# Two Mamba2-like mixers on one core: C·B by blocks, block totals by a product with ones, running sums of two chunks side by side

## The chip, the cores and the metric

The kernel runs on one core of a Trainium2 chip. The metric is the device time of one execution in microseconds (us), lower is better. The engines of the core work side by side, each through its own instructions in order: PE (TensorE, matrix products and transposes), DVE (VectorE), ACT (ScalarE), POOL (GpSimd) and SP (SyncE, which here only issues DMAs). All data are float32; a float32 product shows as two weight loads and two passes in the trace, a transpose as one of each.

## The reference

The input x is (4, 1024, 512): four sequences of 1024 rows. Four layers follow one another, each with a layer norm ahead of it and a residual around it: mixer a, a gated feed-forward layer (ffn), mixer b, the same ffn again.

```python
x = x + mixer_a(layernorm(x))
x = x + ffn(layernorm(x))
x = x + mixer_b(layernorm(x))
x = x + ffn(layernorm(x))
```

Both mixers project x to a gate z (1024 wide), to h (1024), B and C (N each) and to dt (one per head), convolve h, B and C over four rows, apply silu, and run a linear recurrence over the rows. Mixer a has 16 heads of 64 with a state of N = 64; mixer b has 64 heads of 16 with N = 128. The recurrence as mixer b has it:

```python
dt = softplus(dt + dt_bias)
a = -exp(A_log) * dt                 # per row and head; decay exp(a)
state = state * exp(a) + outer(dt * h, B)
y = state @ C + D * h
...
mixer_a: out = norm_w * rms_norm(y * silu(z)) @ out_proj
mixer_b: out = norm_w * rms_norm(y) * silu(z) @ out_proj
```

Mixer a's reference is already written in blocks of 64 rows: within a block y = ((C·Bᵀ) * L) @ (dt h), with L the exponentials of differences of the running sums of a; from block to block a state is carried, which decays by the exponential of the block's total of a.

## The kernel before

**Tiles.** The 4096 rows are 32 chunks of 128 (P), 8 (NCH) to a sequence. Two chunks (GC = 2) make a group, so each mixer has 16 groups. A chunk has two blocks (NQ = 2) of 64 rows (BL). Constants that differ: mixer a has NH = 16, N = 64, SH = P // N = 2, HP = 32, NE = 2·NH + NQ·NH/SH = 48; mixer b has NH = 64, N = 128, SH = 1, HP = 64, NE = 256.

**Order.** `mixer()` emits its work under a manual schedule: PE, DVE, ACT and POOL run exactly in the order in which the Python code emits, only SP's queue is arranged by a scheduler. The loop over groups steps through two generators: `chunk(f, c, following)` for the two chunks of the present group, and `front(ahead, behind)`, which projects the next group. A planner adds up the microseconds that `chunk` yields and emits pieces of `front` until they are paid.

**The pieces of front.** `gate(n)`, n = 0 to 7, projects z in halves of a PSUM bank; after each second one ACT takes a tanh (`tz`, L585), and DVE makes `z` (L590) when the list `later_on` is run, after the next piece. `convolve(j)` projects one tile of h, B or C for both chunks (259 columns, L389), ACT makes the first tap into `u` (L519), DVE adds three (L523); `silu` follows one piece later (tanh L530; L533 writes B as `Bc`, L537 C as `Cc`, L543 h). The first convolution pieces are those of B and C. From the seventh piece on each piece also takes one step of `softplus` (L593 to L651): the steps make dt, then `a` (L619, L620), then a split of `a` in a coarse and a fine part (`parts`, L627, L628), and two steps on the running sums `pcs` of both chunks (L633), their negative as float32 `ncs` and as float16 `two` (ACT, L644, L645), the rest of the float16 pair (DVE, L646), and four DMAs on SP's queue (L650).

**Small steps.** A list `small` holds small PE steps; `large` (L388) pops one behind each large projection product. `prologue(f, c)` puts 13 steps there for a chunk: `sums_of(0)` C·B into a PSUM tile `misc` (L796), `sums_of(1)` and `(2)` running sums of `a` within the block (products with the masks `le_b` and `gt_b`, L798), `sums_of(3)` the blocks' totals of `a` (products with the mask `block`, L805), `sums_of(4)` the transpose of B (L814), with ACT's `ea` = exp of all sums (L816) and the copy `Bt` (L818) and DVE's `Gm`, C·B under the causal mask (L822); then 8 transposes of h (L771), with DVE's dt·h (`hdt`, L775) and ACT's skip D·h (L789). The steps of a group's chunk 0 are deferred at `gate(7)` of the front before it, those of chunk 1 at the start of chunk 0.

**A chunk.** `chunk` makes on POOL the decayed copies of the state (L1005 with its kin), in `decays` the exponents of L by PE (`seg`, L862, L874) and their exponential by ACT (L886, tile `L_b` in mixer b); `weigh` multiplies by Gm on DVE (L893); `to_state` is PE's `pst` (L991) with DVE's additions to the carried states (`Sq` L1000 and L1002, `S` L1025) and POOL's decay between (L1010); `from_state` is PE's `po` (L930) and DVE's `yo` (L941); `open_y` turns yo back (L953), `inner` adds the inside of the blocks (L908), and `close_y` adds D·h (L971), gates on POOL (L977) and takes squares on ACT (L976, L980). `tail` is the output projection `pout` (L722), the sum of squares `ssq` (L731), a copy on ACT (L741) and the residual (L748).

PSUM in a mixer is one pool `mm` of eight banks, taken in rotation. In mixer b the last six groups also carry the end of the first ffn for their rows (`last_steps`). The weights' scaling `weigh_rows` runs on ACT behind the first front.

## Time and profile before

| | us |
|---|---|
| runs of the kernel before | 2763.74, 2763.35, 2756.45 (median 2763.35) |
| the profiled execution | 2760.33, its span 2758.5 |
| mixer a's middle, 60 to 1080 of the span (1020 us) | PE busy 985.5, DVE 747.0, ACT 388.5, POOL 284.7 |
| mixer b's middle, 1330 to 2520 (1190 us) | PE 1144.5, DVE 940.0, ACT 490.1, POOL 365.8 |
| one group of mixer a, 358.5 to 424.4 (65.9 us) | PE 64.0, DVE 48.7, ACT 25.4 |
| an early group of mixer b, 1658.4 to 1734.4 (76.0 us) | PE 75.1, DVE 59.5, ACT 32.0 |
| a late group of mixer b, 2132.3 to 2215.5 (83.2 us) | PE 76.1, DVE 67.1, ACT 33.3 |

The granted TensorE clock is 0.97 to 0.99 of full in the three long stretches. How to read the profile: a line of a timeline has the start in us from the start of the span, the time over which the instructions listed (xN) stretch, the engine, the line of the kernel, the operation, `output<-inputs` with their shapes, and in square brackets how long the engine had been idle just before and whose end released it. For PE the shape ahead of the sizes (`64*128`) is the tile of the array that is used, rows by columns. Pass ends on PE are modelled, so the intervals from start to start are the firmer number. A line of the waits names the waiting instruction, the releaser, the total of the idle time, the number of waits and the longest, in us. Names ending in `_a` and `_b` belong to the mixers, `_f` to the ffn.

### The profile page before, as it was taken

The page shows a single profiled execution, that of the slowest core. Times are in us where ns is not written, and L with a number is a line of the kernel's source. Part 1 is how long each engine was busy: PE and PEld are TensorE (multiplying, and loading weights), DVE is VectorE, ACT ScalarE, POOL GpSimd, SP SyncE. Part 2 cuts the span into 40 slices and gives each one's busy share as a digit, 9 for nine tenths or more (in the row PEclk, how much of TensorE's full clock was granted, in tenths as well). Part 3 has the DMA queues.
Part 4 walks back from the last instruction along what each step waited for, and adds up shares of the span by engine and source line. Part 5 has one row for each costly group of instructions (what it writes and reads, how often), then busy time and mean ns, then how long its engine had stood idle before and what let it go on. Part 6 is the DMA issues. An engine that isn't in the chain of part 4 may idle for free.

```text
span 2758.5 us, 59105 instructions
## 1 busy us (share of the span) xinstructions
PE 2613.9 (95%) x23636; PEld 1682.3 (61%) x23642; DVE 2006.6 (73%) x4493; ACT 1109.5 (40%) x2618; POOL 856.0 (31%) x955
## 2 busy tenths in 40 slices
PE   7999999999999998998999999999999998998897
PEld 6666666666666664345766666666666656665243
DVE  6677777777777775267877777778877778876359
ACT  3333333343433333355434434444434434333246
POOL 1222222222222223053232312322333323324049
PEclk9999999999999999999999999999999999999899
DMA  3000000000000004452000000000000000002424
GB/s 133 11 18 18 18 19 18 22 22 18 18 18 18 15 11 144 175 191 77 12 20 21 23 23 15 23 23 23 24 24 28 19 26 30 11 13 97 175 74 145
DMA packets 93009, 125.09 MB, mean 45 GB/s; under 512 B 38728, under 2 KB 42328, under 8 KB 92736
## 3 DMA queue, kind: packets, MB, share of 16 engines
q1 hardware_dynamic: 80960, 98.23, 11.0%
q10 hardware_dynamic: 9792, 16.82, 1.7%
q0 software_dynamic: 1984, 6.26, 0.7%
q8 instruction: 188, 3.08, 0.5%
q14 instruction: 85, 0.70, 0.1%
HBM read 84.54 MB, written 36.72 MB: 44 GB/s over the span
## 4 chain that ended last, share of the span: by engine, by line
PE 38%; DVE 17%; issue 2%; ACT 2%; POOL 1%; DMA 1%; SPq 0%; DVEq 0%; POOLq 0%; ACTq 0%
PE pc_b L389 7%; PE pz_b L389 7%; PE pout_b L722 6%; PE g_ps L1307 5%; DVE u_b L523 3%; PE py_b L908 2%; DVE L_b L893 2%; PE po_b L930 2%; PE pst_b L991 1%; PE d_ps L1262 1%; DVE no L1443 1%; PE seg_b L862 1%; PE d_ps L1229 1%; PE pd_b L552 1%; PE tph_b L771 1%
## 5 line engine op out<-in xcount | busy, mean ns | idle before, releaser
L389 PE MATMUL pc_b<-xnT_b,w_in_b 128*128 128x259 f32 x1280 | 349.2, 398 | 11.6 <-DVE h_b L971 9.0
L523 DVE SCALAR_TENSOR_TENSOR u_b<-pc_b,cw_b,u_b 128x256 f32<-128x256 f32 x480 | 231.7, 483 | 130.2 <-ACT u_b L519 118.3
L523 DVE SCALAR_TENSOR_TENSOR u_a<-pc_a,cw_a,u_a 128x256 f32<-128x256 f32 x432 | 208.6, 483 | 153.9 <-ACT u_a L519 142.5
L389 PE MATMUL pc_a<-xnT_a,w_in_a 128*128 128x259 f32 x1152 | 319.2, 400 | 0.0
L389 PE MATMUL pz_a<-xnT_a,w_in_a 128*128 128x256 f32 x1024 | 296.7, 406 | 13.3 <-DVE z_a L590 12.6
L389 PE MATMUL pz_b<-xnT_b,w_in_b 128*128 128x256 f32 x1024 | 292.6, 399 | 4.0 <-ACT xnT_b L485 4.0
L389 PEld LDWEIGHTS pc_b<-xnT_b,w_in_b 128*128 128x128 f32 x1280 | 220.9, 192 | 94.6 <-issue 36.5
L1307 PE MATMUL g_ps<-gw,xnT_f 128*128 128x512 f32 x512 | 246.9, 616 | 9.7 <-ACT xnT_f L1300 4.8
L389 PEld LDWEIGHTS pc_a<-xnT_a,w_in_a 128*128 128x128 f32 x1152 | 195.1, 190 | 73.7 <-ACT th_a L530 12.2
L722 PE MATMUL pout_b<-w_out_b,h_b 128*128 128x512 f32 x512 | 231.9, 607 | 0.4 <-POOL h_b L977 0.4
L722 PE MATMUL pout_a<-w_out_a,h_a 128*128 128x512 f32 x512 | 227.5, 597 | 1.0 <-POOL h_a L977 1.0
L389 PEld LDWEIGHTS pz_a<-xnT_a,w_in_a 128*128 128x128 f32 x1024 | 171.1, 193 | 60.2 <-issue 21.8
L389 PEld LDWEIGHTS pz_b<-xnT_b,w_in_b 128*128 128x128 f32 x1024 | 170.4, 192 | 43.8 <-issue 9.5
L977 POOL TENSOR_TENSOR h_b<-h_b,z_b 128x256 f32<-128x256 f32 x128 | 103.2, 827 | 289.1 <-ACT sq_b L976 289.1
L722 PEld LDWEIGHTS pout_b<-w_out_b,h_b 128*128 128x128 f32 x512 | 98.9, 196 | 112.9 <-issue 110.3
L1307 PEld LDWEIGHTS g_ps<-gw,xnT_f 128*128 128x128 f32 x512 | 92.2, 193 | 121.0 <-issue 107.9
L893 DVE TENSOR_TENSOR L_b<-L_b,Gm_b 128x1024 f32<-128x1024 f32 x128 | 163.9, 1322 | 1.0 <-ACT L_b L886 1.0
L519 ACT ACTIVATE u_a<-pc_a,cb_a,cw_a 128x256 f32<-128x256 f32 x144 | 80.7, 560 | 206.8 <-PE pc_a L389 206.8
L519 ACT ACTIVATE u_b<-pc_b,cb_b,cw_b 128x256 f32<-128x256 f32 x160 | 90.1, 563 | 183.1 <-PE pc_b L389 183.0
L722 PEld LDWEIGHTS pout_a<-w_out_a,h_a 128*128 128x128 f32 x512 | 96.3, 191 | 110.4 <-issue 105.5
L1005 POOL TENSOR_TENSOR S_b<-Sq_b,ea_b 128x512 f32<-128x512 f32 x56 | 58.1, 1058 | 337.9 <-DVE Sq_b L1002 281.0
L977 POOL TENSOR_TENSOR h_a<-h_a,z_a 128x256 f32<-128x256 f32 x128 | 107.4, 859 | 165.7 <-DVE rs_a L747 109.7
(365 smaller groups left out, 5068.4 us busy)
## 6 DMA issues: line engine op xcount, KB each, us to landing
d<-in_L_ffn_d_w SPq DMA_DIRECT2D x4, 2048.0 KB
x_f<-xa SPq DMA_DIRECT2D x32, 256.0 KB
xb<-x_b ACTq DMA_DIRECT2D x32, 256.0 KB
x_f<-xb SPq DMA_DIRECT2D x32, 256.0 KB
x_a<-in_L_attn_a_x SPq DMA_DIRECT2D x30, 256.0 KB
xa<-x_a ACTq DMA_DIRECT2D x30, 256.0 KB
out<-x_f SPq DMA_DIRECT2D x22, 256.0 KB
xf<-x_f SPq DMA_DIRECT2D x20, 256.0 KB
```

Source lines behind the costliest of these rows:

```text
L389: nc.tensor.matmul(*args, **kw)
L519: nc.scalar.activation(u, ps[:, 0:GT], AF.Identity, bias=cb[:, j : j + 1], scale=cw[:, j, 0:1])
L523: nc.vector.scalar_tensor_tensor(u, ps[:, k : k + GT], cw[:, j, k : k + 1], u, ALU.mult, ALU.add)
L552: nc.tensor.matmul(pds[c][:, :NH], xnT[:, k, HIST + c * P : HIST + (c + 1) * P], w_in[:, k, m.dt0 : m.dt0 + NH], start=(k == 0), stop=(k = ...
L722: nc.tensor.matmul(pout, f.hs[e // 4][:, e % 4, cols], w_out[:, e, :], **on)
L771: nc.tensor.transpose(tp[:, q * P : (q + 1) * P], f.hs[half][:, q, cols], ident)
L893: nc.vector.tensor_mul(Lr, Lr, Gm.unsqueeze(1).to_broadcast([P, 2 * NS * HB, BL]))
L908: nc.tensor.matmul(py[b][cg * CT : (cg + 1) * CT, e % 4, :], hdt[at, h // HC, u : u + HC, :], Ls[half][at, r, t % NS, hq, :], start=not st ...
L930: nc.tensor.matmul(po[at], Cc[rows, c * P + b * BL : c * P + (b + 1) * BL], S[rows, hsl], start=True, stop=True, skip_group_check=True,)
L977: nc.gpsimd.tensor_mul(yh, yh, zs[half * 2 + r][:, :, cols])
L1005: nc.gpsimd.tensor_mul(heads_of(S2[:, hsl]), heads_of(S1[:, hsl]), over_head(over, P, 512 // HD))
L1307: nc.tensor.matmul(ps, xnT[:, k, :], gw[:, k, :], start=(k == 0), stop=(k == KD - 1 and bias is None))
```

## The change

- The constants `le` (triangle over 128 rows) and `block` (one mask per block) go; `le_b`, the triangle within each block, is built directly, its off-diagonal quarter cleared on POOL.
- B of a group, `Bc`, moves to two fixed buffers of all 128 partitions, used in turn; in mixer a, where B has 64 rows, POOL clears them once, so that the other 64 rows stay zero.
- Two fixed buffers `apart` hold `a` with one column set per block, zero in the rows of the other block. They are cleared once on POOL; for each group two ACT copies, emitted right behind `a` in `softplus`, write the blocks' rows.
- The running sums `pcs` now start anew in each block (`le_b` in place of `le`). In mixer a the two chunks go to two halves of the partitions of the same 128 columns (in place of 64 partitions by 256 columns), and `ncs` and `two` are made on 128 by 128. In mixer b the shape stays. The DMAs are four per group as before.
- In mixer a step 0 of the prologue makes C·B as two products, one per block (64 by 64 each), and the blocks' totals as two products of ones with `apart`; step 3, with its four products, goes, so the prologue has 12 steps. In mixer b C·B stays, and step 3 is one product of ones with `apart` over all 128 output rows in place of two with `block`.
- The transpose of B covers all 128 partitions of `Bc` in both mixers. `Gm` uses `le_b`.
- `sign`, the scale of `ncs` and `two`, alternates over all 128 rows; `st_x` has one buffer in place of two.

The order of emission shifts with it. PE in mixer a: the products of step 0 stand in one slot; the step after `gt_b` is the transpose, one slot earlier than before, and the turns of h follow one slot earlier. ACT in mixer a: `ea` and `Bt` of chunk 1 stand before the `u` behind which they stood, and those of chunk 0 before `tz` of gate 7; the two copies to `apart` stand before the copy of `pout` (L741). ACT in mixer b: the two copies stand between `tz` (L585) and the four exponentials of L (L886). DVE in mixer a: `Gm` stands before the taps of u (chunk 1) and before `z` (chunk 0); in mixer b DVE's order is unchanged but for the constants. POOL: four clears at the start of mixer a, two at the start of mixer b.

```diff
     nc.vector.memset(ones, 1.0)
-    le = const.tile([P, P], F32, tag="le", name="le")
+    le_b = const.tile([P, P], F32, tag="le_b", name="le_b")
     nc.gpsimd.affine_select(
-        out=le, in_=ones, compare_op=ALU.is_ge, fill=0.0, base=0, pattern=[[1, P]], channel_multiplier=-1
+        out=le_b, in_=ones, compare_op=ALU.is_ge, fill=0.0, base=0, pattern=[[1, P]], channel_multiplier=-1
     )
+    nc.gpsimd.memset(le_b[:BL, BL:], 0.0)
     gt_b = const.tile([P, P], F32, tag="gt_b", name="gt_b")
...
-    le_b = const.tile([P, P], F32, tag="le_b", name="le_b")
-    nc.vector.tensor_copy(le_b, le)
-    nc.vector.memset(le_b[:BL, BL:], 0.0)
-    block = const.tile([P, NQ, P], F32, tag="block", name="block")
-    nc.vector.memset(block, 0.0)
-    for q in range(NQ):
-        nc.vector.memset(block[q * BL : (q + 1) * BL, q, :], 1.0)
     neg_half = const.tile([P, 1], F32, tag="neg_half", name="neg_half")
...
             ]
+            Bcs = [wk.tile([P, GT], F32, tag=f"Bc{i}", name=f"Bc_{m.name}_{i}") for i in range(2)]
+            aparts = [wk.tile([P, GC, NQ, NH], F32, tag=f"apart{i}", name=f"apart_{m.name}_{i}") for i in range(2)]
+            for t in (*aparts, *(Bcs if N < P else ())):
+                nc.gpsimd.memset(t, 0.0)
             if HC > 1:
...
             nc.vector.memset(sign, -1.0)
-            nc.vector.memset(sign[HP : 2 * HP], -LO_SCALE)
+            for p0 in range(HP, P, 2 * HP):
+                nc.vector.memset(sign[p0 : p0 + HP], -LO_SCALE)
...
-                f.Bc = wk.tile([N, GT], F32, tag="Bc", name=f"Bc_{tag}", bufs=2)
+                f.Bc, f.apart = Bcs[(f.b * NCH // GC + f.g) % 2], aparts[(f.b * NCH // GC + f.g) % 2]
                 f.Cc = wk.tile([P, GT], F32, tag="Cc", name=f"Cc_{tag}", bufs=2)
...
                         if j == KE:
-                            nc.vector.scalar_tensor_tensor(f.Bc, th[:N], 1.0, u[:N], ALU.add, ALU.mult)
+                            nc.vector.scalar_tensor_tensor(f.Bc[:N], th[:N], 1.0, u[:N], ALU.add, ALU.mult)
                         if j == m.c_tile:
...
                     nc.vector.tensor_scalar(a, a, A_MIN * A_SCALE, 1.0 / A_SCALE, ALU.max, ALU.mult)
+                    for b in range(NQ):
+                        at = slice(b * BL, (b + 1) * BL)
+                        nc.scalar.copy(f.apart[at, :, b, :], a[at])
...
                     pcs = mm(f"pcs_{tag}")
+                    apart = P // (2 * HP)
                     for c in range(GC):
+                        r0, n0 = c % apart * 2 * HP, c // apart * P
                         nc.tensor.matmul(
-                            pcs[: 2 * HP, c * P : (c + 1) * P],
+                            pcs[r0 : r0 + 2 * HP, n0 : n0 + P],
                             parts[:, c, :, :].rearrange("p i h -> p (i h)"),
-                            le,
+                            le_b,
                             start=True,
                             stop=True,
+                            skip_group_check=True,
                         )
-                    rows = slice(0, 2 * HP)
+                    wide = GT // apart
                     ncs = wk.tile([P, 512], F32, tag="t2k", name=f"ncs_{tag}", bufs=TB)
-                    two = wk.tile([P, 2, GT], F16, tag="two", name=f"two_{tag}")
-                    nc.scalar.activation(ncs[rows, :GT], pcs[rows, :GT], AF.Identity, scale=sign[rows])
-                    nc.scalar.activation(two[rows, 0], pcs[rows, :GT], AF.Identity, scale=sign[rows])
-                    nc.vector.tensor_sub(two[rows, 1], ncs[rows, :GT], two[rows, 0])
+                    two = wk.tile([P, 2, wide], F16, tag="two", name=f"two_{tag}")
+                    nc.scalar.activation(ncs[:, :wide], pcs[:, :wide], AF.Identity, scale=sign)
+                    nc.scalar.activation(two[:, 0], pcs[:, :wide], AF.Identity, scale=sign)
+                    nc.vector.tensor_sub(two[:, 1], ncs[:, :wide], two[:, 0])
                     f.cs = dram.tile([GC, 2 * HP // 4, 2, 4, P], F16, tag="cs", name=f"csd_{tag}")
...
                         for j in range(2):
-                            nc.sync.dma_start(f.cs[c, :, j], two[rows, j, c * P : (c + 1) * P])
+                            r0, n0 = c % apart * 2 * HP, c // apart * P
+                            nc.sync.dma_start(f.cs[c, :, j], two[r0 : r0 + 2 * HP, j, n0 : n0 + P])
                     yield
...
                     misc = got["misc"]
-                    if q == 0:
-                        nc.tensor.matmul(misc[:, :P], f.Bc[:, cols], f.Cc[:N, cols], start=True, stop=True)
+                    n0 = P + 2 * NH
+                    if q == 0 and SH == 1:
+                        nc.tensor.matmul(misc[:, :P], f.Bc[:, cols], f.Cc[:, cols], start=True, stop=True)
+                    elif q == 0:
+                        alone = dict(start=True, stop=True, skip_group_check=True)
+                        for b in range(NQ):
+                            at = slice(b * BL, (b + 1) * BL)
+                            own = slice(c * P + b * BL, c * P + (b + 1) * BL)
+                            nc.tensor.matmul(misc[at, at], f.Bc[:, own], f.Cc[:, own], **alone)
+                        for i in range(SH):
+                            heads = slice(i * NH // SH, (i + 1) * NH // SH)
+                            to = misc[i * N : i * N + N, n0 : P + NE].rearrange("p (b h) -> p b h", b=NQ)
+                            nc.tensor.matmul(to, ones[:, :N], f.apart[:, c, :, heads], **alone)
                     elif q < 3:
...
                     elif q == 3:
-                        for b in range(NQ):
-                            for i in range(SH):
-                                n0 = P + 2 * NH + b * (NH // SH)
-                                nc.tensor.matmul(
-                                    misc[i * N : i * N + N, n0 : n0 + NH // SH],
-                                    block[:, b, :N],
-                                    f.a[:, c, i * NH // SH : (i + 1) * NH // SH],
-                                    start=True,
-                                    stop=True,
-                                    skip_group_check=True,
-                                )
+                        nc.tensor.matmul(
+                            misc[:, n0 : P + NE], ones, f.apart[:, c].rearrange("p b h -> p (b h)"), start=True, stop=True
+                        )
                     else:
-                        nc.tensor.transpose(misc[:, P + NE : P + NE + N], f.Bc[:, cols], ident[:N, :N])
+                        nc.tensor.transpose(misc[:, P + NE : P + NE + P], f.Bc[:, cols], ident)
                         ea = sm.tile([P, NE], F32, tag="ea", name=f"ea_{tag}", bufs=2)
...
                             at = slice(b * BL, (b + 1) * BL)
-                            nc.vector.tensor_mul(Gm[at], misc[at, at], le[at, at])
+                            nc.vector.tensor_mul(Gm[at], misc[at, at], le_b[at, at])
                         f.early[c] = Gm, ea, Bt
-                return [lambda q=q: sums_of(q) for q in range(5)] + [
+                return [lambda q=q: sums_of(q) for q in range(5) if q != 3 or SH == 1] + [
                     lambda half=half, q=q: turn(half, q) for half in range(2) for q in range(4)
```

More of the change, by code (lines that the diff above doesn't have):

```diff
@@ L439, in measure @@
                 def measure(c):
-                    st = sm.tile([P, 6], F32, tag="st_x", name=f"st_{tag}_{c}")
+                    st = sm.tile([P, 6], F32, tag="st_x", name=f"st_{tag}_{c}", bufs=1)
                     nc.vector.bn_stats(st, f.xs[c])
```

## The prediction

> **What bounds the kernel now.** Three views are read in this order. The page's list of engines says which engine is short of time:

> ```profile
> PE 2613.9 (95%) x23636; PEld 1682.3 (61%) x23642; DVE 2006.6 (73%) x4493; ACT 1109.5 (40%) x2618; POOL 856.0 (31%) x955
> ```

> TensorE is busy for 95% of the span, but its ends are modelled, so the waits are read next: consumer on the left, the releaser behind the arrow, then total idle, count and longest, in us.

> ```profile
> PE py_a L953 <- DVE yo_a L941: 19.8, 17, 2.0
> PE pz_a L389 <- DVE z_a L590: 12.6, 14, 1.4
> PE po_b L930 <- DVE Sq_b L1002: 10.1, 13, 2.3
> ```

> Once in nearly every group of two chunks PE stands still for a VectorE result. Such a wait absorbs whatever PE saves before it, as far back as the last point where DVE or ScalarE had waited for PE. The timeline of one group of mixer a (358.5 to 424.4 in the neighbouring one: 65.9 us, PE busy 63.97) shows that stretch for chunk 1:

> ```profile
> 335.34 0.49 PE L796 MATMUL misc_a<-Cc_a,Bc_a 64*128 64x128 f32 x2
> ...
> 336.30 0.29 PE L798 MATMUL misc_a<-a_a,le_b 128*128 128x16 f32 x2
> ...
> 337.71 0.41 PE L805 MATMUL misc_a<-a_a,block 128*64 128x8 f32 x8
> 337.82 0.56 ACT L519 ACTIVATE u_a<-pc_a,cb_a,cw_a 128x256 f32<-128x256 f32 x1 [9.30 <-PE pc_a L389]
> ...
> 338.42 1.52 DVE L523 SCALAR_TENSOR_TENSOR u_a<-pc_a,cw_a,u_a 128x256 f32<-128x256 f32 x3 [7.98 <-ACT u_a L519]
> ...
> 341.76 0.69 DVE L1025 TENSOR_TENSOR S_a<-S_a,pst_a 128x512 f32<-128x512 f32 x1 [1.22 <-POOL S_a L1005]
> 342.37 0.45 DVE L822 TENSOR_TENSOR Gm_a<-misc_a,le 64x64 f32<-64x64 f32 x2
> ...
> 346.61 0.43 PE L953 MATMUL py_a<-ident,yo_a 64*128 64x64 f32 x4 [1.19 <-DVE yo_a L941]
> ```

> The anchor is 337.82: ACT and DVE had waited 9.30 and 7.98 for PE's convolution product. From there DVE, POOL and DVE run on without PE until the wait of 1.19 at 346.61. Chunk 0 has the like, anchored at 377.06 (end of PE's transposes of x) and ending in z:

> ```profile
> 387.14 0.58 ACT L585 ACTIVATE tz_a<-pz_a 128x512 f32<-128x512 f32 x1
> ...
> 387.76 0.69 DVE L590 SCALAR_TENSOR_TENSOR z_a<-tz_a,pz_a 128x512 f32<-128x512 f32 x1 [2.24 <-ACT tz_a L585]
> ...
> 388.50 0.70 PE L389 MATMUL pz_a<-xnT_a,w_in_a 128*128 128x256 f32 x2 [0.82 <-DVE z_a L590]
> ```

> The third timeline is a late group of mixer b (2132.3 to 2215.5: 83.2 us, PE 76.11, DVE 67.07):

> ```profile
> 2130.70 0.58 ACT L585 ACTIVATE tz_b<-pz_b 128x512 f32<-128x512 f32 x1
> 2131.18 2.05 ACT L886 ACTIVATE L_b<-seg_b 128x512 f32<-128x512 f32 x4
> 2133.09 0.60 ACT L519 ACTIVATE u_b<-pc_b,cb_b,cw_b 128x256 f32<-128x256 f32 x1
> ...
> 2141.51 0.23 DVE L620 TENSOR_SCALAR a_b<-a_b 128x128 f32<-128x128 f32 x1
> ...
> 2143.91 1.52 DVE L523 SCALAR_TENSOR_TENSOR u_b<-pc_b,cw_b,u_b 128x256 f32<-128x256 f32 x3
> ...
> 2150.05 1.28 DVE L1002 TENSOR_TENSOR Sq_b<-Sq_b,pst_b 128x512 f32<-128x512 f32 x2
> ...
> 2150.78 0.64 PE L930 MATMUL po_b<-Sq_b,Cc_b 128*64 128x512 f32 x1 [1.10 <-DVE Sq_b L1002]
> ```

> ACT did the four exponentials and u 8.4 us before `a` existed on DVE.

> **What mixer a's products save.** Start-to-start intervals price a slot between large products (one fp32 pass of 256 columns 0.22 us). The C·B slot from 335.34 lasts 334.81 to 336.30 less four passes, 0.61; block 337.71 to 338.05, 0.34; the transpose at 341.02 has 0.37. After: C·B and totals go as eight passes on two column halves, like block's eight, about 0.54 (at most 0.72, where the halves do not overlap); block is gone; the transpose, full width, costs 0.11 (its row in b, 1483.10 to 1483.21). The running sums need 0.58 for four passes on one half (374.02 to 374.60); on two halves two passes fewer, −0.2. Per group that is 0.2 + 2 × (0.07 + 0.34 + 0.26), about 1.5; I take 1.35, since part of the 0.26 is a switch of tile shape that moves to the neighbour.

> [...] Here the row-tiled slot took 0.61 and mixer b's full-array C·B 0.22 (1476.42 to 1477.52 less 0.88), so the row speaks for the padding in a lone small product. [...]

> **How much of it arrives.** Chunk 1: only what lies before 337.82 counts. C·B gives −0.07. But the transpose and ACT's exp (ea) and copy (Bt) now stand before u: u comes 0.32 later (two small ACT rows 0.21 each, partly under the waiting). Against it Gm, 0.48 from 342.37 to the taps at 342.85, leaves the chain, as it is done while DVE idles its 7.98. Net −0.07 + 0.32 − 0.48 = −0.23. The other PE saving only lengthens 1.19. Chunk 0: ea and Bt stand before tz at 387.14, +0.2, and the running sums lie ahead of the anchor, −0.2. So −0.23 per group, 15 groups: −3.4 us. Bounds: −7 (ea and Bt hidden) to +3 (halves in series, 0.18 × 15 more, and u fully 0.42 late). What is late next is yo, then py; nothing else.

> **The copies of `a` (ACT).** Two per group; the nearest row is a 128-element ACT exp at 0.21 pitch (1296.48 to 1296.69), bounded by 0.3 (the skip copies of L789). In a they wait at most 0.63 for DVE and put the pout copy about 1 us back; ACT's next result that PE needs comes at 370.72, so I cost them 0 there; without that cover, 0.4 × 15 = 6.

> In b they are put between tz (2130.70) and the exponentials (2131.18). The engine works in order, so it now stands until 2141.74, when `a` ends. Queued behind are the four exponentials, u, th and the layer norm's scaling: DVE's taps and weighing wait for them, and PE's seg banks stay taken longer. At `a`'s end: semaphore 0.05 + copies 0.42 + from the first exponential to u 1.91 (2131.18 to 2133.09) + u until the taps 0.58 = 2.96, against the 2.17 that DVE needs for its own work from `a` to the taps (2141.74 to 2143.91). So the taps come 0.79 late (0.97 with copies of 0.3). DVE is unbroken from there to Sq at 2150.05, and PE already waits for Sq (1.10; in early groups 0.13 to 0.4), so 0.79 passes to PE whole. ACT's lead over `a` is 7.1 us in 8 groups, 10.6 in 6, 8.2 in one: nowhere small. 15 groups × 0.79 = 11.9; bounds 0 (weighing and taps could have slack) to 0.97 × 16 = 15.5. The running sums' fp16 `two` on ACT is 1.4 late too, which puts PE's ssq (2146.66) back 1.36, but within the wait for Sq.

> **Mixer b's products.** Totals: one full-array product in place of two column-tiled ones, 0.48 to 0.31, −0.17 per chunk. It lies ahead of po's wait, so 0; if PE were the limit in the eight early groups, −0.17 × 2 × 8 = −2.7.

> **Prologues.** The first group of each mixer has no cover: copies wait 1.57 in a (+0.5) and 3.2 in b (+0.6): +1.1.

> **At nothing.** Constants, the memsets on POOL (about 0.22 each, from 2.69 for 3072 elements) under its 19.5 idle (1272.2 to 1291.7): +0.9 without it. `ncs` and `two` are half as wide in a (DVE 0.41 to about 0.3), with 0.79 idle behind. SP's queue issues the same four DMAs per group; one load of the masks' past rows stands one place earlier, past none that is late. Two fixed buffers for B follow the same alternation as two rotating ones.

> **Sum.** −3.4 + 11.9 + 1.1 = +9.6. The profiled execution took 2760.33 (span 2758.5), so 2769.9; the median of the runs, 2763.35, lies 3.0 above it, so 2773.

> **Rivals.** (1) The stall grows: mm banks rotate over eight, the seg banks are free only at about 2144.2 instead of 2133.1, and pst (2143.09) wants them; with ssq's 1.36 counting in full the price is 1.36 × 15 = 20.4, and the time 2763.4 + 20.4 + 1.1 − 3.4 = 2781.5, about 2782. For: pst follows pcs at once. Against: banks come free one by one, 0.5 apart, as pst takes them. (2) The stall is hidden: DVE's 2.17 after `a` hides nearly all if the taps have slack, leaving 2763.4 − 3.4 = 2760. For: DVE is busy only 67 of 83 us. Against: no idle gap on DVE from 2130.5 to 2151.3. (3) The other side, faster: PE's saving arrives, 1.35 × 15 = 20 in a and 5 in b, since PE is 97% busy in a's group. With the stall, 2763.4 − 25 + 13 = 2751; without, 2738. It decides if the chains from the anchors shift with PE; against it speak the waits 19.8 and 12.6. (4) That C·B's halves do not overlap adds 0.18 × 30 = 5.4 at most, within the range.

> **Chances.** Forecast 0.54 (own range 2766 to 2779), rival (1) 0.12, (2) 0.16, (3) 0.18. The range 2760 to 2786 takes in (1), half of (2) and the bounds, and leaves out (3). This kernel's measurement can tell 0.3%, 8.3 us: same is 2755.1 to 2771.6. Faster 0.20 (all of (3) and a tail of (2)); same 0.30 (the rest of (2) and the forecast's lower end); slower 0.50.

> **What would show it.** Right: in b ACT idle 7 to 10.6 before the copies, released by DVE's `a`; a DVE gap of about 0.8 before the taps; po's wait about 0.8 longer in early groups; groups of b 76.8 and 84.0 (now 76.0 and 83.2), of a 65.7. Wrong: no DVE gap there; groups of a at 64.5, their waits for yo and z gone; or pst waiting for ACT's exponentials.

## The result and the profile after

The changed kernel took 2772.47 to 2781.66 us in four runs, median 2778.18, beside 2762.06 for four runs of the kernel before on the same occasions. The ratio is 1.0060, with a 95% interval of 1.0037 to 1.0083: slower by 0.4 to 0.8%. Its profiled execution took 2772.47, with a span of 2770.8 (before: 2760.33 and 2758.5).

To see where the time went, the start of the first z (DVE) of each group in the two profiles is compared. Up to the first z of mixer b the changed kernel gains 12.7 us (1272.4 in place of 1285.1), and through mixer b it loses 24.4 (the last z comes at 2504.4 in place of 2492.7). A group is called undisturbed if the trace's clock records show no half clock in it (the clock is the second thing below). An undisturbed group of mixer a takes 65.03 us in place of 65.87. An early group of mixer b takes 77.1 (undisturbed) or 78.5 (with a stretch of half clock) in place of 75.9 to 76.0, a late one 84.4 to 84.9 in place of 83.2.

The page's list of engines, and the waits of PE that were shown of before:

```profile
PE 2605.9 (94%) x23508; PEld 1674.4 (60%) x23514; DVE 2002.3 (72%) x4489; ACT 1121.1 (40%) x2682; POOL 859.0 (31%) x962
```

```profile
PE py_a L962 <- DVE yo_a L950: 24.2, 17, 2.1
PE pz_a L388 <- ACT tz_a L584: 14.7, 14, 1.3
...
PE po_b L939 <- DVE Sq_b L1011: 5.5, 11, 1.1
```

PE has 8 us less to do, and its wait for yo has grown by 4.4 in all. In mixer a's group (timeline of the changed kernel, the same group and places as before, all engines) the new order shows:

```profile
332.95 0.21 ACT L825 ACTIVATE ea_a<-misc_a 128x48 f32<-128x48 f32 x1 [9.34 <-PE misc_a L823]
...
333.15 0.58 ACT L518 ACTIVATE u_a<-pc_a,cb_a,cw_a 128x256 f32<-128x256 f32 x1
333.30 0.46 DVE L831 TENSOR_TENSOR Gm_a<-misc_a,le_b 64x64 f32<-64x64 f32 x2 [7.76 <-ACT Bt_a L827]
...
333.78 1.52 DVE L522 SCALAR_TENSOR_TENSOR u_a<-pc_a,cw_a,u_a 128x256 f32<-128x256 f32 x3
...
341.39 0.46 PE L962 MATMUL py_a<-ident,yo_a 64*128 64x64 f32 x4 [1.48 <-DVE yo_a L950]
...
381.83 0.61 ACT L584 ACTIVATE tz_a<-pz_a 128x512 f32<-128x512 f32 x1
...
382.47 0.69 DVE L589 SCALAR_TENSOR_TENSOR z_a<-tz_a,pz_a 128x512 f32<-128x512 f32 x1
382.58 0.67 PE L388 MATMUL pz_a<-xnT_a,w_in_a 128*128 128x256 f32 x2 [1.05 <-ACT tz_a L584]
...
383.21 0.40 PE L551 MATMUL pd_a<-w_in_a,xnT_a 128*128 128x16 f32 x2
```

Gm now runs in DVE's idle stretch before the taps, and ea and Bt run ahead of u. PE waits 1.48 for yo here (1.19 before), and 1.39 to 1.48 in the groups of mixer a from 100 to 1030 us. Behind tz, PE starts the next projection at 382.58, only 0.11 after the start of z, where before it stood until z had ended.

In a late group of mixer b (timeline of the changed kernel, ACT, then DVE and PE):

```profile
2135.81 0.58 ACT L584 ACTIVATE tz_b<-pz_b 128x512 f32<-128x512 f32 x1
2146.88 0.60 ACT L622 COPY apart_b<-a_b 64x128 f32<-64x128 f32 x2 [10.49 <-DVE a_b L619]
2147.51 2.06 ACT L895 ACTIVATE L_b<-seg_b 128x512 f32<-128x512 f32 x4
2149.60 0.56 ACT L518 ACTIVATE u_b<-pc_b,cb_b,cw_b 128x256 f32<-128x256 f32 x1
...
2150.20 1.52 DVE L522 SCALAR_TENSOR_TENSOR u_b<-pc_b,cw_b,u_b 128x256 f32<-128x256 f32 x3 [1.10 <-ACT u_b L518]
...
2148.16 0.71 PE L637 MATMUL pcs_b<-le_b,parts_b 128*128 128x128 f32 x4 [3.40 <-ACT L_b L895]
2148.80 3.51 PE L1000 MATMUL pst_b<-S_b,Bt_b 64*128 64x512 f32 x8
...
2157.08 0.64 PE L939 MATMUL po_b<-Sq_b,Cc_b 128*64 128x512 f32 x1 [0.64 <-DVE Sq_b L1011]
```

ACT stands 10.49 us until DVE has `a`; the exponentials and u stand behind the copies, and DVE idles 1.10 before the taps, where before it had no gap. PE's running sums, too, now wait for an exponential to free its bank. In the kernel before they waited for DVE at this place, and the products `pst` behind them took less time:

```profile
2142.48 0.68 PE L633 MATMUL pcs_b<-le,parts_b 128*128 128x128 f32 x4 [2.83 <-DVE parts_b L628]
2143.09 1.99 PE L991 MATMUL pst_b<-S_b,Bt_b 64*128 64x512 f32 x8
```

The second thing the profile shows is the TensorE clock. The trace's clock records know two levels, full and half, and within the span the half lasts 3.41 us or a multiple. One such stretch lies on the `pst` above (granted clock 0.50 from 2149.2 to 2152.4), which is why it takes 3.51 in place of 1.99. In mixer b (1330 to 2500 of the span) such stretches add up to 54.6 us in the changed kernel and 23.9 in the one before. The mean granted clock of the four runs is 0.974 to 0.978, that of 75 of 86 later runs of the kernel before 0.981 to 0.987.

### The profile page after: what moved, and what is told of

Read it like the earlier page. It is cut to its first block, busy times and chain, and to the rows that moved or that the text cites. A ratio compares the mean times of both kernels' runs of the same rounds, so it can differ in the third digit from the quotient of the medians.

```text
span 2770.8 us, 58908 instructions
## 1 busy us (share of the span) xinstructions
PE 2605.9 (94%) x23508; PEld 1674.4 (60%) x23514; DVE 2002.3 (72%) x4489; ACT 1121.1 (40%) x2682; POOL 859.0 (31%) x962
## 4 chain that ended last, share of the span: by engine, by line
PE 31%; DVE 21%; ACT 4%; issue 3%; POOL 1%; DMA 1%; SPq 0%; ACTq 0%; POOLq 0%; DVEq 0%
PE g_ps L1316 6%; PE pz_b L388 5%; PE pc_b L388 4%; PE pout_b L728 4%; DVE u_b L522 4%; DVE L_b L902 2%; PE po_b L939 2%; PE pst_b L1000 1%; ACT L_b L895 1%; DVE h_b L542 1%; PE d_ps L1271 1%; DVE v_b L613 1%; PE py_b L917 1%; DVE h_b L980 1%; PE d_ps L1238 1%
## 5 line engine op out<-in xcount | busy, mean ns | idle before, releaser
L388 PE MATMUL pc_b<-xnT_b,w_in_b 128*128 128x259 f32 x1280 | 356.2, 404 | 13.7 <-DVE h_b L980 9.1
L1316 PE MATMUL g_ps<-gw,xnT_f 128*128 128x512 f32 x512 | 245.7, 613 | 10.2 <-DMA gw<-in_L_ffn_gate_w 5.5
L895 ACT ACTIVATE L_b<-seg_b 128x512 f32<-128x512 f32 x256 | 131.1, 597 | 22.8 <-PE seg_b L883 22.5
```

What stands on the lines that cost most here:

```text
L388: nc.tensor.matmul(*args, **kw)
L895: nc.scalar.activation(L[:, r], sg[r0 + r], AF.Exp)
L1316: nc.tensor.matmul(ps, xnT[:, k, :], gw[:, k, :], start=(k == 0), stop=(k == KD - 1 and bias is None))
```

## The experiments

Each kernel was timed beside the kernel before on the same chip; ratios are to it, with 95% intervals. The sets stand on several chips, so kernels of different sets are better compared by their ratios than by their medians. Beside the ratio two numbers are used. "Lost clock" is a run's time x (1 - its mean granted clock), averaged over a kernel's runs. "Base" is the time without what goes with lost clock: over all 204 runs of this study a line was fitted with one slope for all and one level for each kernel; the slope is 0.79 us of time for each us of lost clock, and a run lies 2.5 us from the line (one standard deviation). The fit treats the clock as a cause; that is tested below, and so is the one slope, which turns out to be an average of places where a microsecond of lost clock cost 0.99 us and places where it cost 0.09.

| kernel | median us | ratio | base | lost clock | group a | early b | late b |
|---|---|---|---|---|---|---|---|
| before (four sets of runs) | 2758.7 to 2761.8 | 1 | 2722 to 2725 | 46 to 49 | 65.87 | 76.0 | 83.2 |
| the change | 2778.2 | 1.0060 (1.0037 to 1.0083) | 2726 | 65 | 65.03 | 78.5 (77.1 undisturbed) | 84.7 |
| copies late in b | 2753.2 | 0.9984 (0.9968 to 1.0001) | 2712 | 54 | 65.02 | 75.7 | 83.2 |
| copies alone, on before | 2781.5 | 1.0086 (1.0065 to 1.0107) | 2739 | 55 | 65.9 | 77.0 | 84.7 |
| mixer a's part alone | 2755.4 | 0.9982 (0.9967 to 0.9997) | 2713 | 54 | 65.02 | 75.8 | 83.2 |
| mixer b's part alone | 2785.1 | 1.0096 (1.0077 to 1.0115) | 2738 | 59 | 65.87 | 78.4 (77.0 undisturbed) | 84.5 |
| a's sums alone, on before | 2757.2 | 0.9999 (0.9985 to 1.0013) | 2720 | 50 | 65.66 | 75.9 | 83.2 |
| a's part, empty step | 2785.5 | 1.0088 (1.0062 to 1.0113) | 2726 | 74 | 67.2 (65.6 undisturbed) | 75.9 | 83.2 |
| empty step, filled | 2757.1 | 0.9976 (0.9960 to 0.9993) | 2724 | 42 | 65.59 | 75.8 | 83.4 |
| copies late, filled | 2747.7 | 0.9953 (0.9935 to 0.9970) | 2712 | 44 | 65.03 | 75.7 | 83.3 |

Groups are the median of 13, 5 and 5 periods from z to z in the profile.

**Is it ACT's stall in mixer b?** Three runs, each with one idea: move the copies, put them alone into the kernel before, and put copies there that wait for nothing.

```diff
 # copies late: in mixer b behind the fp16 pair of the running sums
-                    for b in range(NQ):
-                        nc.scalar.copy(f.apart[at, :, b, :], a[at])
...
                             nc.sync.dma_start(f.cs[c, :, j], two[r0 : r0 + 2 * HP, j, n0 : n0 + P])
+                    for b in range(NQ):
+                        nc.scalar.copy(f.apart[at, :, b, :], a[at])
 # copies alone, on the kernel before, mixer b only
+                        nc.scalar.copy(spare[at], a[at])
 # copies of a constant, same place
+                        nc.scalar.copy(spare[at], Ab[at].unsqueeze(1).to_broadcast([BL, GC, NH]))
```

> The change with one edit in mixer b: the two ACT copies of a are emitted behind the running sums' fp16 pair, three pieces later, instead of right behind a. Nothing is left out. Stall theory (the copies hold up ACT's four exponentials and u until DVE has a; measured in the changed kernel: ACT idle 130.8 us before the copies in 16 groups, taps of u 1.03 late per group): ACT's idle before the copies goes, an early group of b falls from 77.1 to about 75.8, a late one from 84.5 to about 83, the kernel from 2778 to about 2750, 0.4 to 0.5% under the kernel before. Rival (the totals by a product with ones, or the running sums that restart in each block, cost b its time): groups of b stay at 77 to 78.5 and the time at 2778, +0.6%.

> The kernel before with only the two ACT copies of a in mixer b, at the place where the change has them; they write a tile that nothing reads, and st_x has one buffer to make room for it. Stall theory: groups of b lengthen by about 1.1 to 1.2 (early) and 1.2 to 1.6 (late), plus the stretches of half TensorE clock that the new idle brings; in all +20 to +28, so 2782 to 2790, 0.7 to 1.0% over the kernel before. Rival (products or sums are the cause): within 0.2% of the kernel before, at most 16 x 0.6 = 10 us if the copies only add their own time.

> The kernel before with two ACT copies in mixer b at the place of the change's copies, but of the constant rates instead of a, so that they wait for nothing; they write a tile that nothing reads. It separates the copies' own 0.6 us of ACT from the wait for a. Stall theory: ACT has 7 to 10 us idle behind, so nothing: within 0.15% of the kernel before, groups of b 76.0 and 83.3. Rival (ACT's own time counts): 16 x 0.6 = 10 us, +0.35%.

With the copies late, mixer b is back at its old periods, as expected, and the kernel at 0.9984; 0.4 to 0.5% under the kernel before was expected, and the next experiment shows where the rest went. ACT's timeline in an early group of this kernel shows why:

```profile
1722.65 0.58 ACT L584 ACTIVATE tz_b<-pz_b 128x512 f32<-128x512 f32 x1
1723.13 2.04 ACT L900 ACTIVATE L_b<-seg_b 128x512 f32<-128x512 f32 x4
1725.04 0.59 ACT L518 ACTIVATE u_b<-pc_b,cb_b,cw_b 128x256 f32<-128x256 f32 x1
...
1734.65 0.46 ACT L651 ACTIVATE two_b<-pcs_b,sign_b 128x256 f16<-128x256 f32 x1
1735.01 0.59 ACT L661 COPY apart_b<-a_b 64x128 f32<-64x128 f32 x2
```

The exponentials follow tz at once, and the copies run where `a` has long been there. The copies alone slow the kernel before by 0.65 to 1.07%, as the change's whole part in b does (0.77 to 1.15%). In its waits of ACT stands the same stall as in the change:

```profile
ACT spare_b L625 <- DVE a_b L621: 130.7, 16, 10.5
```

The copies of a constant, equal in work, follow tz at once:

```profile
1730.05 0.58 ACT L586 ACTIVATE tz_b<-pz_b 128x512 f32<-128x512 f32 x1
1730.53 0.59 ACT L625 COPY spare_b<-Ab_b 64x128 f32<-64x128 f32 x2
1731.14 2.06 ACT L891 ACTIVATE L_b<-seg_b 128x512 f32<-128x512 f32 x4
```

They give 1.0002 (0.9990 to 1.0014). So the wait is what costs, not ACT's 0.6 us, and not the products or sums.

**Do the two mixers add up?** In mixer a's part alone the totals of b stay with `block`; in mixer b's part alone a stays as it was.

```diff
 # mixer a's part alone: the change, but
+                    if SH == 2:
                         for b in range(NQ):
...
                     elif q == 3:
-                        nc.tensor.matmul(
-                            misc[:, n0 : P + NE], ones, f.apart[:, c].rearrange("p b h -> p (b h)"), start=True, stop=True
-                        )
+                        for b in range(NQ):
+                            for i in range(SH):
...
+                                    block[:, b, :N],
...
 # mixer b's part alone: the kernel before, with copies and totals of the change where SH == 1
```

> The change in mixer a alone; in mixer b the totals come from products with the block masks as before and no copies of a are made (the running sums there restart in each block, as in the change, which alters no instruction's shape). If a's gain (measured 12.7 us from the start to the first z of mixer b) stands by itself: 2762 - 13 = 2749, 0.45% under the kernel before, groups of a 65.0, groups of b 76.0 and 83.3 as before. If the gain in a is bought by b's loss (shifted clock or transfers): about 2760 to 2765.

> The change in mixer b alone (copies of a at their place, one buffer for them, totals by a product with ones); mixer a as before, but for le_b in place of le. Stall theory: as the copies alone, less at most 0.17 x 2 x 8 = 3: +18 to +26, so 2780 to 2788. If the two mixers' effects add, this time less the kernel before plus that of mixer a alone gives the change's own +16. Rival (clock chance: a's shorter groups put b's waits at worse moments): clearly under +15.

They add: 2713 - 2724 = -11 and 2738 - 2724 = +14 in base, against the change's +2 (all bases against 2724, the middle of the four sets of before). But of a's 11 us only some 4 arrive in the median (0.9982), because lost clock grew from 47 to 54 us: 7 x 0.79 = 5.5 are given back. The expectation of 2749 missed by that, and so did that of the late copies, whose lost clock is 54 as well.

**What makes mixer a's 0.84 per group?** The running sums were put alone into the kernel before; and in a's part alone the place of the removed step was kept as a step that issues nothing.

```diff
 # empty step
+                    elif q == 3 and SH == 2:
+                        return
-                return [lambda q=q: sums_of(q) for q in range(5) if q != 3 or SH == 1] + [
+                return [lambda q=q: sums_of(q) for q in range(5)] + [
```

> The kernel before with one part of the change: mixer a's running sums of the two chunks side by side on 128 by 128 (and the scale column that this needs); nothing else. Step as in the prediction: two passes fewer per group ahead of an anchor, 0.21 per group, a group of a 65.87 - 0.21 = 65.66, in all -3; a clear difference in the times is not to be had from 3 us. Rival (the sums lie on no path, the 0.21 is swallowed by the wait for z): groups stay at 65.87.

> Mixer a's part of the change alone, as in the run of mixer a alone, but the place of step 3 is kept in the queue of small steps as a step that issues nothing, so the transpose of B, ea, Bt, Gm and the turns of h stay where they were. It separates PE's removed work from the changed order. Order theory (of 0.84 per group the order makes most: Gm out of the chain -0.21, one turn fewer behind the wait for yo -0.17, Gm and z in the other order -0.22; the sums -0.21): groups of a at 65.5 to 65.66, time about 2755 to 2760. Rival (the removed products make it): groups stay at 65.03.

The sums give 0.21 per group, as expected (65.66). With the empty step the undisturbed groups take 65.6. So 0.57 of the 0.84 come from the place of the steps, and the removed products by themselves give no more than 0.27, sums included. What was not expected is the time: +0.88%, although its undisturbed groups are shorter. PE's waits in this kernel have grown (to 1.7 for yo and 1.5 for z in a usual group):

```profile
PE py_a L978 <- DVE yo_a L966: 28.1, 17, 2.0
PE pz_a L392 <- DVE z_a L594: 21.0, 14, 2.0
```

and behind one of them, of 1.47 for z, the granted clock falls to 0.50. First PE's timeline, then the windows of the same stretch (the last numbers of a window are granted clock, DMA share and GB/s):

```profile
666.39 0.70 PE L392 MATMUL pz_a<-xnT_a,w_in_a 128*128 128x256 f32 x2 [1.47 <-DVE z_a L594]
...
667.07 0.68 PE L392 MATMUL pz_a<-xnT_a,w_in_a 128*128 128x256 f32 x2
...
669.03 1.20 PE L392 MATMUL pz_a<-xnT_a,w_in_a 128*128 128x256 f32 x2
```

```profile
660.00:668.00 8.00, 6.53 (x59) 5.31 (x58) 5.58 (x17) 4.96 (x17) 2.68 (x5) 0.98 0.23 71
668.00:672.00 4.00, 4.00 (x13) 3.46 (x14) 2.71 (x4) 1.24 (x5) 3.40 (x2) 0.50 0.02 4
672.00:676.00 4.00, 4.00 (x13) 3.37 (x13) 0.17 (x1) 0.60 (x1) 0.00 (x0) 0.50 0.00 0
```

The same pair of passes takes 1.20 in place of 0.68. The clock records of half speed here are 3.41, 6.83, 10.24 us long and so on, the granted clock in them is 0.50, and waits of 1.4 to 2.0 us stand right before these stretches.

**Is the clock the cause, or a companion?** PE was given work in those waits whose result nothing reads. If the clock follows PE's idleness, more work must make the kernel faster. The number of products is 3 unless the expectation names another.

```diff
 # filled (mixer a): before the wait for yo, into the half bank that the next gate overwrites
+                    if n == 2 and SH == 2:
+                        for k in range(3):
+                            nc.tensor.matmul(
+                                pz[:, GT:], w_in[:, k, m.z0 : m.z0 + P], xnT[:, k, HIST:], start=True, stop=True, skip_group_check=True
+                            )
 # before the wait for z, into the free half of the last seg bank
+                    if SH == 2 and c == 0:
+                        for k in range(3):
+                            nc.tensor.matmul(
+                                whole[3][:, 256:], w_in[:, k, :P], w_in[:, k, :256], start=True, stop=True, skip_group_check=True
+                            )
```

> The run with the empty step (mixer a's part alone, old order of the small steps; +0.88%) plus filling work on PE whose results nothing reads: three products of 256 columns per group before the wait for yo (1.7 us there) and three before the wait for z at a group's start (1.5 us). Nothing is left out. Clock theory (the empty step's loss of 26 us is half TensorE clock brought on by these two waits: 74 us of lost clock against 47 in the kernel before): groups of a 65.5 to 65.7 as in its undisturbed groups, no half-clock stretch between 130 and 1030, time 2753 to 2762, so 22 us or more faster for doing more work. Rival (the old order itself is slow, by waits or banks that the span hides): stays at 2775 to 2790.

> The change with the late copies in mixer b, plus three products of 256 columns (six passes, 1.3 us) per group in mixer a whose result is overwritten, put right before PE's wait for yo (1.48 us in the changed kernel), so that PE stands still for about 0.2 there instead. Clock theory (PE's longer single waits of about 1.4 to 1.6 bring stretches of half TensorE clock, seen right behind such waits at 449 and 869 us of the late-copies profile, none in the kernel before between 69 and 1062): groups of a keep 65.03, no half-clock stretch between 100 and 1030, mean granted clock up by about 0.002 to 0.003, time 3 to 8 us under that of the late copies (2754.8 mean), so 2747 to 2752. Rival (half-clock stretches come with the load and not with the waits): the clock does not rise, and the time stays or grows by what the products stick out.

> Control: the kernel before with two filling products per group of mixer a before the wait for yo (1.19 us, so about 0.3 is left). Clock theory with a bound between the waits of 1.2 and those of 1.5: the kernel before has no half-clock stretch there to remove, so within 0.15% of the kernel before, groups of a 65.87. Rival (the filling speeds the kernel up by something other than the clock's stretches, such as a faster restart of PE): groups shorter than 65.8, time 3 to 8 us lower.

> The change with the late copies in mixer b plus one filling product per group of mixer a before the wait for yo, so that PE stands still for about 1.05 us there (1.48 without, 0.2 with three). If waits above 1.2 to 1.4 us bring the half clock: as with three products, 2744 to 2751, no half-clock stretch between 100 and 1030. If the chance of one falls evenly with the idle time: between, about 2750 to 2753, with stretches left.

> The change with the late copies in mixer b, three filling products before mixer a's wait for yo and two (0.87 us) before its wait for z at a group's start (1.0 to 1.6 us); nothing is left out, the fillings' results are not read. Clock theory: no half-clock stretch between 100 and 1030 in any run, lost clock about 40 to 44 us (44 with the first filling alone), groups of a 65.03, time 2742 to 2748, 0.45 to 0.65% under the kernel before. Rival (the second filling delays ACT's exponentials of L through their bank, or the load keeps the clock down): 2750 or more.

The empty step with fillings falls from 2785.5 to 2757.1, with groups of 65.59 as in its undisturbed ones. The windows from 130 to 1030 of the empty step without and with the fillings:

```profile
130.00:1030.00 900.00, 858.19 (x6158) 581.37 (x6158) 631.84 (x1519) 338.72 (x910) 242.45 (x283) 0.97 0.06 18
```

```profile
130.00:1030.00 900.00, 892.72 (x6508) 606.20 (x6508) 657.43 (x1581) 348.78 (x936) 247.82 (x292) 1.00 0.06 18
```

PE is busier by 35 us, the clock is whole (56.4 us of half clock in this window without, none with), and the kernel goes from 0.88% over the kernel before to 0.24% under it, with more work. That shows the clock to be a cause. The change with late copies gains by three fillings, too: 2747.7 and 0.9953, lost clock 44 in place of 54, at the same base. With both waits filled it is 2748.0 (0.9944 to 0.9975), just outside the expected 2742 to 2748, with the narrowest spread of all (2746.4 to 2749.6). The control, fillings on the kernel before, changes nothing (1.0006, 0.9988 to 1.0024; lost clock 51), as expected. Not expected were two stretches of 13.65 us in mixer a of its profile, each behind a wait of 1.39 for z, a wait that the control does not fill. One filling in place of three does not help (2759.1, 0.9985; lost clock 58; two stretches of 10.24 us behind waits of 1.54 and 1.57 for z, which it does not fill either); the expectation named 2753 at most.

**When does a wait bring the half clock?** The length of a single wait does not decide it: in the empty step PE waits 1.73 to 1.82 for yo in each of thirteen groups between 100 and 1030 us, and one of these waits is followed by half clock. The clock records say more. In each of the fourteen profiles all of them begin on one grid of 3.41 us. Between 100 and 1030 us the clock fell from full to half 17 times in all, each time at the end of a window of this grid in which PE had stood still for 1.37 to 1.95 us. Of the 3760 windows with full clock behind which it stayed full, 25 had as much idle time, and only seven, all of the empty step, more than 1.40 (up to 1.74). So it matters in mixer a whether a wait falls whole into one window: of 32 waits of at least 1.37 that lay whole in one, 15 were followed by half clock, of 56 that lay across an edge, 2. The bound is not sharp, and in mixer b, among many small products, it does not hold (the clock fell behind windows with 0.4 to 2.5 us of idle time): what decides there was not shown.

**What does lost clock cost?** It depends on the place. In the changed kernel a group of mixer a with a stretch of 3.41 us takes 66.77 in place of 65.03; in the kernel before an early group of mixer b with one takes 77.52 in place of 75.9 to 76.0. But late groups of mixer b in the kernel before take 83.24 with one and 83.22 without. Fitted over the groups of all fourteen profiles, a microsecond of lost clock (two of half clock) costs 0.99 us in mixer a and in early groups of b, and 0.09 in late groups. The late group shown for the change tells why: PE's wait for Sq takes up the longer `pst` (0.64 left of 1.10), and DVE's chain up to Sq sets the time there. The slope of 0.79 mixes the two. Where a kernel's extra lost clock lies in late groups, as in the change and in the copies alone (37.5 us of half clock there in both profiles, 17.1 in the kernel before), the base is too low and the clock's share too high. No run fills PE's waits in mixer b; what the clock costs there rests on this comparison of groups.

## Why the prediction was right, and where not

**The sign and the place: right.** "In b they are put between tz and the exponentials. The engine works in order, so it now stands until 2141.74": the profile shows ACT idle 7.06 in early and 10.49 in late groups (predicted 7 to 10.6), DVE with a new gap before the taps, and the copies alone carry the whole loss of mixer b.

**Its size: mis-sized.** 0.79 per group was predicted for the taps. In the early group from 1692 they came 1.19 late against the work ahead of them and 1.03 against the group, since 0.17 that the totals' product saved did arrive there (it was taken as 0). A copy has a pitch of 0.31 (two from 2146.88, exponentials at 2147.51) and not the 0.21 of the row taken, just above the bound of 0.3 from the nearest copies; and u starts 2.09 behind the first exponential, not 1.91. The term was 11.9, and 12.5 with the first group. In base the stall costs 15; read from the profiles by groups it is more, an estimate of 18 to 20: mixer b's growth from its first to its last z (24.4 in the change, 17.1 with the copies alone), less half of the extra half clock in its early part (10.2 more in the change, 6.8 less with the copies alone) and less 0.9 for that in its late groups.

**Mixer a: "−0.23 per group" failed.** Measured: -0.84. The split that follows is read from the timelines; experiments separate only the place of the steps (0.57), the sums (0.21) and the rest. The step for chunk 1 held, -0.21: ea and Bt push u back (0.24), Gm leaves the chain. Three things were missed. "The other PE saving only lengthens 1.19": no, one turn of h has moved from behind that wait to before it, which is worth 0.19 behind the wait. For chunk 0 "ea and Bt stand before tz, +0.2" is true of ACT, but not of PE: PE's first projection there now waits for tz and not for the end of z, and the group gains 0.22 in place of nothing. The likeliest reason is the bank that the pool hands out (PE's next wait, of pd, is now the one for z); this was read from the trace only. And the sums gave their 0.21 without being cancelled. The bound "+3" on this term does not follow from its parts either: on −3.4, 0.18 × 15 for halves in series and 0.10 × 15 for u come to +0.8.

**The clock: not in the sum.** The sum took a wait as a loss of its own length and saved work before a wait as nothing. Lost clock rose from 47 to 65 us in the mean of the runs, which at 0.79 would be +14. That is too much, since part of it lies in the late groups: in the two profiles lost clock grew by 15.7 us, 10.2 of them in late groups of b, so that some 5 or 6 of the measured +16 are the clock's (an estimate from one profile each). The empty step shows the error best: PE work removed before a wait cost 27 us, and filling the wait brought them back.

**The total.** Predicted was -3.4 + 13.0 = +9.6. The two profiles differ by 12.3: -12.7 up to the first z of mixer b, +24.4 through mixer b (the stall, and some 5 or 6 of clock), +0.6 behind it. The medians differ by 16.1. By the table, -11 (a) + 14 (b) in base and +14 for lost clock make +17; this adds up, but the one slope moves a part of the stall's cost into the clock's. The forecast of 2773 lies near the measured 2778.2 by luck: the gain missed in a (some 8 to 9 us) makes up for most of what was missed in b's stall and in the clock. Only b's term was right for its reason, and it was too small.

**The rivals.** That PE's saving arrives (3) was half right in a, where it came by order and not by work, and did not decide. Of (1) the wait is real, PE's running sums wait for an exponential (3.40); but this is only 0.57 longer than their wait before (2.83), and po's wait for Sq shrinks by nearly as much (1.10 to 0.64); late groups lost 1.2 to 1.7, clock included. (2), a hidden stall, is refuted by the copies alone. Of the markers, "po's wait about 0.8 longer in early groups" was wrong: PE itself came late there, having waited for the seg banks.

## What to carry to other kernels

On an engine that works in order, a copy costs what it makes the instructions behind it wait (ACT stood 7.06 to 10.49 us ahead of two copies of 0.31 each): ask when its input is ready, and put it behind the last instruction that could run earlier; here that is worth 0.76% (from 1.0060 to 0.9984), some 21 us, at the same work. Where PE stands at a wait in every group, less work before it is not free of cost: in the empty step half clock followed waits of 1.4 to 2.0 us, lost clock was 74 us in place of 47, and work that filled the waits brought the time from 2785.5 to 2757.1. What a microsecond of lost clock costs depended on the place: 0.99 us in mixer a and in early groups of mixer b, 0.09 in its late groups, where DVE's chain sets the time. Work taken out of a queue of small steps also moves all steps behind it; look at what now stands before and behind the waits, as that made two thirds of the gain in mixer a.
